# Layer 2 of a four-layer image network, written as two streams instead of one

## The chip, the cores and the metric

The kernel runs on one core of a Trainium2 chip. The metric is the device time of one execution in microseconds (us); smaller is better. Engines are named as in the profile: PE (matrix multiply) and PEld (its weight loads), DVE (vector engine), ACT (activation engine), POOL (GpSimd, which here issues the indirect DMAs), SP (which issues all other DMAs).

## What is computed

Sixteen images of 192 channels and 32x32 pixels pass through four layers, each with a group norm in front and a residual sum behind. Only layer 2, a deformable depthwise convolution, is touched; the others share its engines.

```python
# layer 2: x = x + deform(groupnorm(x))
offset = conv3x3(x, w_off) + b_off            # 18 numbers per pixel: 9 taps, (dy, dx)
py = row + ky + offset[:, :, 0]; px = col + kx + offset[:, :, 1]
for yi, xi, wgt in four_corners(floor(py), floor(px)):   # bilinear sampling
    acc += gather(x, clip(yi) * W + clip(xi)) * (wgt * valid)
out = einsum('bckhw,ck->bchw', acc, w_def)    # 9 taps, one weight per channel and tap
```

Layer 0 is a gated recurrence with a convolution, layer 1 an attention whose queries and keys come from a small simulated circuit, layer 3 a gated feed-forward block with a 2x2 transform and a depthwise 3x3 convolution.

## The kernel before

The small circuit's tables come first, then phase A (layer 0), until about 3290 us. The rest is phase B, where layers 1 to 3 of different images run side by side. It is written as Python generators. Each emits the instructions of its part and now and then yields a number, the planned cost of what it has emitted. `weave` (from line 83) holds for each stream a plan time, starts it at the stream's third number, takes a step of the stream whose plan time is smallest, and adds the step's cost divided by the stream's second number. One unit of plan time is therefore one image in every stream; it is called a *unit* below. The framework's scheduler then orders each engine's queue: the emission order is the priority, and an instruction that is ready while an engine is free may go ahead of one that isn't. On the chip, each queue is in order.

There are four streams in phase B before the change:

- `vectors` (from line 959), 87.0 a unit, start 0: the residual of layer 0, group norm, the circuit's states `psi` (line 1035), `pcirc` (1057), its square `prob` (1059, ACT), `pz` (1069).
- `attention` (1110), 205.8, start 1.27: per pair of heads, `pmax` (1132, PE), its row maxima `mx` (1164, DVE), `pscore` (1132, PE), `pexp` (1206, ACT), `pav` (1196, PE). `pmax`, `pscore`, `pcirc` and layer 3's `phad` share a PSUM tag `big` of two buffers.
- `layer2` (1272), 169.5, start 2.53: for each image first `layer2_offsets`, then `layer2_gathers`, one after the other.
- `layer3` (1435), 136.9, start 3.81: `phad` (1474), the depthwise taps `dc` (1525, DVE), `pout` (1560).

`layer2_offsets` (49.5 of the 169.5 a unit, with 2 for the tail of the image in front) does the group norm, writes the padded image `xpad`, transposes it into five tiles `xt` (1311) and writes these with 22 DMAs (1298) into a DRAM table `xg`, of which there are two, used in turn; `poffc` (1327) is the offset convolution, 72 matmul records an image; then come 15 short DVE instructions that make the row numbers `ix` (1358) and the four corner weights `w4` (1363).

`layer2_gathers` does 36 steps an image (4 blocks of pixels by 9 taps), each planned at 3.0. A step issues two indirect DMAs (`read`, 1382) two steps ahead into `gt` (six buffers, that is three steps), makes the first corner's product of the next step on ACT (`first`, 1390), adds the other three corners with six DVE instructions (1423), multiplies by the weights of the tap (1425), and adds the result into the PSUM tile `pdef` by a matmul with the identity (1429). After the ninth tap a `tail` copies the block out of PSUM (1395), transposes it (`pdt`, 1403), adds the residual (1406) and stores it to `x3d`, from which layer 3 reads. The tail is emitted with the first tap of the next block; that of the last block after the first step of the next image's offsets.

Tags shared by both halves: `acc` with five buffers (for `acc` and for `xt`), PSUM `mm` with two (`pxt`, `poffc`, `poff`, `pdt`, and the small matmuls of the other streams), `xp` with three (`ot`, the tail's `x2`, and layer 3's `tot` and `xo`), `ix` and `w4` with two each.

Of the kernel before, what the change touches and what calls it, by code (L numbers as in the profile page):

```python
# [52 lines left out]
def groupnorm(nc, pool, mm, cn, x, out):  # L53

    gm, rs = yield from groupstats(nc, pool, mm, cn, x)
    nm = pool.tile([96, 2], F32, tag="gnnm", name="gnnm")
    nc.vector.scalar_tensor_tensor(nm, gm, -1.0, rs, ALU.mult, ALU.mult)
    yield 1.5
    for k in range(2):
        xk = x[k] if len(out[k].shape) == 2 else x[k].rearrange("p (r w) -> p r w", w=32)  # L60
        nc.scalar.activation(out[k], xk, AF.Identity, bias=nm[:, k:k + 1], scale=rs[:, k:k + 1])
# [21 lines left out]
def weave(streams):  # L83


    streams = [[s[2] if len(s) > 2 else 0.0, s[1], s[0]] for s in streams]
    while streams:
        s = min(streams, key=lambda s: s[0])
        try:
            s[0] += next(s[2]) / s[1]  # L90
        except StopIteration:
            streams.remove(s)
# [685 lines left out]
def phase_b(tc, d, out, ydram, stats, cn, nb):  # L778

    nc = tc.nc  # L780
    with ExitStack() as ctx:
# [152 lines left out]


        left = [SimpleNamespace() for _ in range(nb)]
        done = [nb] + [0] * 4
        g = SimpleNamespace(**locals())

        def together(n):  # L940
# [5 lines left out]
        def stream(i, work):  # L946
            for b in range(nb):
                assert done[i] > b
                yield from work(g, b, left[b])
                done[i + 1] = b + 1  # L950


        nc.scalar.preload_act_table_set("natural_log_exp_and_others")

        weave([(stream(0, vectors), 87.0), (attention(g), 205.8, 1.27), (layer2(g), 169.5, 2.53),
               (stream(3, layer3), 136.9, 3.81)])


def vectors(g, b, left):
# [309 lines left out]
    yield from todo.ends  # L1269


def layer2(g):
    late = SimpleNamespace(tail=iter(()))
    for b in range(g.nb):
        assert g.done[2] > b
        yield from layer2_offsets(g, b, g.left[b], late)
        yield from layer2_gathers(g, b, g.left[b], late)
    yield from late.tail


def layer2_offsets(g, b, left, late):


    nc, cn, p1, p2, mm = g.nc, g.cn, g.p1, g.p2, g.mm
    xpad, x = g.xpad, left.x
    xg = g.xg[b % 2]
    norm = groupnorm(nc, p2, mm, cn, [x[:, k, :] for k in range(2)],
                     [xpad[:, k, 1:33, 1:33] for k in range(2)])
    yield next(norm)
    yield from late.tail  # L1290
    yield from norm
    yield 2.0

    def table(xt, cr, u, t0, n, q):

        dst = bass.AP(tensor=xg.tensor, offset=xg.offset + (u + 128 * t0 + q) * 768 + cr * 192,
                      ap=[[768, 128 - q], [128 * 768, n], [1, 192]])
        nc.sync.dma_start(dst, xt[q:])


    flat = xpad.rearrange("p k r w -> p k (r w)")
    for t2 in range(5):
        n = min(2, 9 - t2 * 2)
        pv = mm("pxt")
        for j in range(n):
            o = 4 + (t2 * 2 + j) * 128
            for k in range(2):
                nc.tensor.transpose(pv[:, (j * 2 + k) * 96:(j * 2 + k) * 96 + 96], flat[:, k, o:o + 128],
                                    cn.ident[:96, :96])
        xt = g.pairs("xt")  # L1310
        nc.scalar.activation(xt[:, 0:n, :], pv[:, 0:n * 192].rearrange("p (t c) -> p t c", t=n), AF.Identity)
        for cr, sh in enumerate((0, 1, 34, 35)):
            if sh > 4 and t2 == 0:
                table(xt[:, 0:1, :], cr, 4 - sh, 0, 1, sh - 4)
                table(xt[:, 1:2, :], cr, 4 - sh, 1, 1, 0)
            else:
                table(xt[:, 0:n, :], cr, 4 - sh, t2 * 2, n, 0)
        yield 1.5


    po = mm("poffc")
    for t in range(9):
        dy, dx = t // 3, t % 3
        for k in range(2):
            for hf in range(2):
                q = (k * 2 + hf) * 32
                nc.tensor.matmul(po[q:q + 32, :], g.woff[:, k, t, :],  # L1327
                                 xpad[:, k, hf * 16 + dy:hf * 16 + dy + 16, dx:dx + 32], start=(t == 0), stop=(t == 8))
        yield 2.0
    yield 3.0  # L1330
    ot = g.xp("ot")
    nc.scalar.activation(ot, po, AF.Identity)
    yield 2.0
    pf = mm("poff")
    for j in range(4):
        nc.tensor.transpose(pf[:, j * 128:(j + 1) * 128], ot[:, j * 128:(j + 1) * 128], cn.ident)
    yield 4.0
    n = 144
    pos = p1.tile([128, n], F32, tag="pos", name="pos")
    pfv = pf.rearrange("p (j k f c) -> p k f j c", j=4, k=2, f=2)  # L1340
    posv = pos.rearrange("p (f j c) -> p f j c", f=2, j=4)
    nc.vector.tensor_tensor(posv, pfv[:, 0, :, :, 0:18], g.gridb.rearrange("p (f j) c -> p f j c", f=2), ALU.add)
    nc.vector.tensor_tensor(posv, pfv[:, 1, :, :, 0:18], posv, ALU.add)
    nc.vector.tensor_scalar(pos, pos, -1.0, 32.0, ALU.max, ALU.min)
    fi = p1.tile([128, n], I32, tag="fi", name="fi")
    nc.vector.tensor_copy(fi, pos)
    fl = p1.tile([128, n], F32, tag="fl", name="fl")
    nc.vector.tensor_copy(fl, fi)
    t1 = p1.tile([128, n], F32, tag="t1", name="t1")
    nc.vector.tensor_tensor(t1, fl, pos, ALU.is_gt)  # L1350
    nc.vector.tensor_sub(fl, fl, t1)
    nc.vector.tensor_sub(pos, pos, fl)
    nc.vector.tensor_scalar(t1, pos, -1.0, 1.0, ALU.mult, ALU.add)
    flv = fl.rearrange("p (n c) -> p n c", c=2)
    iv = p1.tile([128, n // 2], F32, tag="iv", name="iv")
    nc.vector.scalar_tensor_tensor(iv, flv[:, :, 0], 34.0, flv[:, :, 1], ALU.mult, ALU.add)
    ix = p2.tile([128, n // 2], I32, tag="ix", name="ix")
    nc.vector.tensor_scalar_add(ix, iv, 35.0)
    w4 = p2.tile([128, 4, n // 2], F32, tag="w4", name="w4")
    pv_ = pos.rearrange("p (n c) -> p n c", c=2)  # L1360
    qv_ = t1.rearrange("p (n c) -> p n c", c=2)
    for cr in range(4):
        nc.vector.tensor_mul(w4[:, cr, :], (pv_ if cr // 2 else qv_)[:, :, 0], (pv_ if cr % 2 else qv_)[:, :, 1])
    left.ix, left.w4 = ix, w4
    yield 6.0
# [202 lines left out]
def network(tc, d, out, nb):  # L1568
    nc = tc.nc
    with ExitStack() as ctx:  # L1570
        cp = ctx.enter_context(tc.tile_pool(name="c_1", bufs=1))
        dp = ctx.enter_context(tc.tile_pool(name="c_d", bufs=1, space=DRAM))
        cn = SimpleNamespace()
        cn.ident = load(nc, cp, d["ident"], "ident")
        cn.g6 = load(nc, cp, d["g6"], "g6")
        const_cols(nc, cp, cn, [("eps5", 1e-5), ("one", 1.0), ("lnsc", -0.5 * math.log(32.0)), ("hpi", math.pi / 2)])
        cn.lqk = cp.tile([128, 2, 128], F32, name="lqk")
        ydram = dp.tile([nb, 192, 2, HS], F32, name="ydram")
        stats = dp.tile([192, nb, 2, 6], F32, name="stats")
        circuits(tc, d, cn)  # L1580
        phase_a(tc, d, ydram, stats, cn, nb)
        phase_b(tc, d, out, ydram, stats, cn, nb)
# [126 lines left out]
```

## Time and profile before

| | |
|---|---|
| median of 3 runs | 9260.08 us (9257.92 to 9267.99) |
| the profiled execution | 9279.24 us |
| its span, first to last instruction | 9277.3 us |
| busy over the span: PE, DVE, ACT, POOL | 85%, 75%, 46%, 20% |
| mean granted TensorE clock | 0.847 |
| first gather of image 0, 2, 13, 15 | 3807.3, 4441.5, 8348.7, 8946.7 us |
| last gather issued | 9116.7 us |
| the attention's last `pexp` | 8835 us |

How to read it: the rows by line give an instruction's busy time over the whole execution, the mean duration of one, and after the second bar the idle time of its engine just before it, with what ended that. A row of a stretch gives the stretch (us from the span's start), its length, then the busy time of PE, PEld, DVE, ACT and POOL with the number of instructions, the granted clock, the DMA engines' busy share and GB/s. A row of the waits says which engine and line waited for what, how long in all, how often, and the longest.

From image 2 to image 13 phase B repeats itself: 11 images between 4441.5 and 8348.7 us, 355.2 us each. Within one such period the first gather to the last takes about 247 us (the *gather stage*), and the rest, about 106 us, in which no gather is issued, is the *offset stage*.

### The profile page before, as it was taken

What the parts mean: (1) busy time and instruction counts of PE and PEld (TensorE: products, weight loads), DVE (VectorE), ACT (ScalarE), POOL (GpSimd) and SP (SyncE); (2) the same over time, 40 slices, a digit from 0 to 9 for tenths busy, and PEclk for the clock granted to TensorE, in tenths of its full rate; (3) what the DMA queues carried; (4) which work ended last, traced back from release to release, by engine and by line L of the source; (5) the groups of instructions that cost most, each with busy time, mean ns of one, the idle gap of its engine ahead of it and who ended that gap; (6) DMA issues with size and microseconds to landing.
All of it is one profiled execution on the core that took longest, in us unless ns stands there. A gap on an engine that the chain in (4) does not pass through costs nothing. (4 is left out here: it accounts for less than half of the span.)

```text
span 9277.3 us, 92108 instructions
## 1 busy us (share of the span) xinstructions
PE 7898.9 (85%) x30512; PEld 3406.5 (37%) x30512; DVE 6930.6 (75%) x14313; ACT 4241.6 (46%) x7405; POOL 1851.5 (20%) x1680
## 2 busy tenths in 40 slices
PE   5999999999999959898888888888888888888843
PEld 2555555555555532233323223323323233232221
DVE  7777777777777743569778778778788778788888
ACT  3444444444444424445444444444444445454432
POOL 0100000101010000222312223223223223223242
PEclk9899999999999968887887888877887878878865
DMA  1111111111111110433333433434334334334342
GB/s 53 42 40 45 47 47 43 45 43 46 44 50 43 42 49 19 132 119 118 121 118 104 127 116 116 124 113 124 114 120 124 110 107 136 109 106 138 121 152 68
DMA packets 303530, 819.62 MB, mean 88 GB/s; under 512 B 48827, under 2 KB 165629, under 8 KB 303051
## 3 DMA queue, kind: packets, MB, share of 16 engines
q0 software_dynamic: 92160, 453.06, 15.7%
q1 hardware_dynamic: 210891, 360.67, 12.9%
q8 instruction: 240, 3.93, 0.2%
q14 instruction: 239, 1.96, 0.1%
HBM read 667.52 MB, written 132.94 MB: 86 GB/s over the span
## 5 line engine op out<-in xcount | busy, mean ns | idle before, releaser
L1382 POOL DMA_INDIRECT gt<-xg,ix x1152 | 1529.3, 1328 | 4259.5 <-DVE acc L1423 1496.2
L1423 DVE SCALAR_TENSOR_TENSOR acc<-gt,w,acc 128x192 f32<-128x192 f32 x3456 | 1210.0, 409 | 246.9 <-ACT acc L1390 243.3
L1132 PE MATMUL pmax<-kt,qt 32*128 32x512 f32 x3072 | 996.4, 863 | 256.4 <-ACT pexp L1206 226.1
L1164 DVE TENSOR_REDUCE mx<-pmax 128x2 f32<-128x1024 f32 x768 | 922.7, 1217 | 328.1 <-PE pmax L1132 327.1
L1390 ACT ACTIVATE acc<-gt,w 128x192 f32<-128x192 f32 x1152 | 503.3, 451 | 1307.6 <-DMA gt<-xg,ix 1084.4
L1196 PE MATMUL pav<-pexp,vo 128*64 128x512 f32 x3072 | 1032.0, 713 | 11.7 <-ACT pexp L1206 11.7
L1206 ACT ACTIVATE pexp<-pscore 128x1024 f32<-128x1024 f32 x768 | 767.6, 1015 | 481.5 <-PE pscore L1132 348.0
L1132 PE MATMUL pscore<-qt,kt 32*128 32x512 f32 x3072 | 807.9, 731 | 166.6 <-DVE mx L1164 105.2
L509 POOL COPY qbd<-qT 32x384 f32<-32x384 f32 x512 | 305.4, 596 | 2838.9 <-PE se L543 2752.1
L1429 PE MATMUL pdef<-acc,ident 128*128 128x384 f32 x1152 | 660.4, 664 | 206.2 <-DVE acc L1425 206.2
L1525 DVE SCALAR_TENSOR_TENSOR dc<-pad,wdw,dc 128x512 f32<-128x512 f32 x1152 | 804.6, 742 | 26.3 <-ACT dc L1523 25.1
L539 ACT ACTIVATE dm<-dm,wtm 128x128 f32<-128x128 f32 x1536 | 490.7, 388 | 347.2 <-DVE dm L495 267.5
L1132 PEld LDWEIGHTS pmax<-kt,qt 32*128 32x128 f32 x3072 | 281.2, 240 | 856.7 <-ACT pexp L1206 458.2
L551 PEld LDWEIGHTS pintra<-v,pt 128*128 128x128 f32 x3072 | 426.0, 212 | 163.3 <-issue 70.0
L1429 PEld LDWEIGHTS pdef<-acc,ident 128*128 128x128 f32 x1152 | 214.7, 231 | 703.4 <-DVE acc L1425 329.9
L1132 PEld LDWEIGHTS pscore<-qt,kt 32*128 32x128 f32 x3072 | 224.9, 204 | 648.2 <-DVE mx L1164 294.3
L551 PE MATMUL pintra<-v,pt 128*128 128x33 f32 x3072 | 435.3, 290 | 2.5 <-DVE pt L546 2.3
L1059 ACT ACTIVATE prob<-pcirc 128x1024 f32<-128x1024 f32 x192 | 195.9, 1023 | 510.2 <-PE pcirc L1057 499.6
L1196 PEld LDWEIGHTS pav<-pexp,vo 128*64 128x64 f32 x3072 | 202.1, 154 | 588.9 <-issue 558.8
L1057 PE MATMUL pcirc<-psiT,lqk 64*128 64x512 f32 x768 | 312.6, 788 | 97.3 <-DVE mx L1164 72.5
L546 DVE SCALAR_TENSOR_TENSOR pt<-se,dm 128x512 f32<-128x512 f32 x384 | 262.9, 685 | 141.1 <-PE se L543 138.0
L1560 PE MATMUL pout<-gelu,wout 128*96 128x512 f32 x512 | 267.7, 673 | 87.0 <-DVE gelu L1548 79.7
(423 smaller groups left out, 12887.5 us busy)
## 6 DMA issues: line engine op xcount, KB each, us to landing
dm<-gd SPq DMA_DIRECT2D x128, 768.0 KB
xg<-xt SPq DMA_DIRECT2D x224, 192.0 KB
gt<-xg,ix POOLq DMA_INDIRECT x1152, 4.5
xb<-x_in SPq DMA_DIRECT2D x32, 384.0 KB
y<-ydram SPq DMA_DIRECT2D x32, 384.0 KB
x1d<-xb SPq DMA_DIRECT2D x32, 384.0 KB
xnd<-y SPq DMA_DIRECT2D x32, 384.0 KB
xn<-xnd SPq DMA_DIRECT2D x48, 256.0 KB
```

The lines of the kernel that those rows point to most:

```text
L539: nc.scalar.activation(dm[:, h, :], dm[:, h, :], AF.Exp, bias=wtm[:, c, 64 + h:65 + h])
L551: nc.tensor.matmul(pa[:, hh * 33:hh * 33 + 33], pt[:, h * 128:(h + 1) * 128], v33[:, hh, :], start=True, stop=True)
L1057: nc.tensor.matmul(pc[:, hh * HS:(hh + 1) * HS], cn.lqk[r, w, :], ps[hf][r, :], start=True, stop=True)
L1132: nc.tensor.matmul(out[j][:, hh * HS:(hh + 1) * HS], lhs(j, r), rhs(j, r), start=True, stop=True)
L1164: nc.vector.tensor_reduce(mx[:, tt, hf, :], pm[hf].rearrange("p (h s) -> p h s", h=2), AX.X, ALU.max, negate=True)
L1196: nc.tensor.matmul(po[0][hh * 64:hh * 64 + 64], vo[:, tt, hh * 32:hh * 32 + 64], pe[:, hh * HS:(hh + 1) * HS], start=(tt == 0), stop=(tt = ...
L1206: nc.scalar.activation(pe, ps[j], AF.Exp)
L1382: nc.gpsimd.indirect_dma_start(out=gt, out_offset=None, in_=xg, in_offset=bass.IndirectOffsetOnAxis(ap=ix[:, c:c + 1], axis=0))
L1390: nc.scalar.activation(acc[:, j, :], gt[:, 0:192], AF.Copy, scale=w4[:, 0, c:c + 1])
L1423: nc.vector.scalar_tensor_tensor(acc[:, j, :], gt[:, cr * 192:(cr + 1) * 192], w4[:, cr, c:c + 1], acc[:, j, :], ALU.mult, ALU.add)
L1429: nc.tensor.matmul(po[:, 0:384], cn.ident, acc.rearrange("p j c -> p (j c)"), start=(t == 0), stop=(t == 8))
L1525: nc.vector.scalar_tensor_tensor(out, src, w, add, ALU.mult, ALU.add)
```

## The change

`layer2` becomes two streams. `offsets` runs `layer2_offsets` image by image; its 49.5 are followed by empty steps of 1.0 up to 140.5, so that its unit is again one image and its work lies in the first 0.352 of the unit. `gathers` runs `layer2_gathers` image by image with 120 a unit: 4 + 36 x 3 + 4 tails x 2. It starts 0.38 units behind `offsets`. The tail of an image's last block is now emitted with the first tap of the next image. `layer3` starts at 3.96 instead of 3.81. No instruction is added or removed.

```diff
-        done = [nb] + [0] * 4
+        done = [nb] + [0] * 5
...
-        weave([(stream(0, vectors), 87.0), (attention(g), 205.8, 1.27), (layer2(g), 169.5, 2.53),
-               (stream(3, layer3), 136.9, 3.81)])
+        weave([(stream(0, vectors), 87.0), (attention(g), 205.8, 1.27), (offsets(g), 140.5, 2.53),
+               (gathers(g), 120.0, 2.91), (stream(3, layer3), 136.9, 3.96)])
...
-def layer2(g):
+def offsets(g):
+
+    for b in range(g.nb):
+        assert g.done[2] > b and g.done[3] + 2 > b
+        spent = 0.0
+        for cost in layer2_offsets(g, b, g.left[b]):
+            spent += cost
+            yield cost
+        g.done[5] = b + 1
+        while spent < 140.0:
+            spent += 1.0
+            yield 1.0
+
+
+def gathers(g):
     late = SimpleNamespace(tail=iter(()))
     for b in range(g.nb):
-        assert g.done[2] > b
-        yield from layer2_offsets(g, b, g.left[b], late)
+        assert g.done[5] > b
         yield from layer2_gathers(g, b, g.left[b], late)
     yield from late.tail
...
-def layer2_offsets(g, b, left, late):
+def layer2_offsets(g, b, left):
...
-    yield next(norm)
-    yield from late.tail
     yield from norm
     yield 2.0
```

## The prediction, made before the changed kernel was run

> **What bounds the kernel now.** I began with the slices of the whole span, to find the part that repeats.
>
> ```profile
> PE   5999999999999959898888888888888888888843
> DVE  7777777777777743569778778778788778788888
> PEclk9899999999999968887887888877887878878865
> ```
>
> Slices 17 to 37 are one flat stretch, PE at eight to nine tenths and DVE at seven to eight: neither is full, so the two hold each other up. Next I cut periods into the stage with gathers and the stage without, and beside these put the first image, at which layer 3 does not run yet, and the end.
>
> ```profile
> 3807.00:4002.00 195.00, 166.32 (x531) 54.51 (x532) 146.84 (x332) 86.10 (x146) 84.58 (x71) 0.75 0.53 165
> 4002.00:4100.00 98.00, 94.34 (x477) 31.53 (x474) 51.76 (x96) 52.52 (x73) 0.99 (x2) 0.97 0.27 79
> 5161.00:5407.00 246.00, 199.19 (x709) 74.42 (x710) 203.22 (x428) 121.40 (x205) 92.21 (x72) 0.83 0.46 140
> 5407.00:5513.00 106.00, 100.27 (x389) 30.84 (x390) 77.75 (x138) 51.24 (x64) 0.61 (x1) 0.81 0.24 71
> 8835.00:9128.00 293.00, 132.22 (x356) 59.22 (x356) 244.89 (x558) 95.89 (x184) 157.53 (x92) 0.60 0.49 154
> ```
>
> In the gather stage (third row) PE is busy 0.81 and DVE 0.83; in the offset stage (fourth) PE 0.95 and DVE 0.73. So the offset stage is PE's, and the gather stage nobody's. What waits in it is in the waits of the third row's stretch, and of the fourth's:
>
> ```profile
> ACT acc L1390 <- DMA gt<-xg,ix: 59.2, 35, 6.2
> PE pmax L1132 <- ACT pexp L1206: 17.3, 6, 5.9
> DVE acc L1423 <- ACT acc L1390: 16.3, 7, 6.3
> ```
>
> ```profile
> DVE psi L1035 <- issue: 19.9, 1, 19.9
> PEld pmax L1132 <- ACT pexp L1206: 3.8, 4, 1.5
> ```
>
> In the gather stage ACT stands 59.2 us with `first` at the head of its queue until a gather lands; `pexp` is queued behind it, and PE's largest wait is for `pexp`. In the offset stage that wait is nearly gone, and DVE stands 19.9 us in one piece while PE runs `poffc`, `pcirc` and `pz` without a gap. The rows by line say that this hole comes in most images (321.0/16 = 20 us) and that POOL's long idle time is mostly behind DVE's tap sums, whose buffers the gathers reuse:
>
> ```profile
> L1035 DVE TENSOR_TENSOR psi<-vec 128x512 f32<-128x512 f32 x96 | 62.2, 686 | 321.0 <-issue 224.8 <-PE pz L1069 80.7 <-ACT gelu L1546 15.4
> L1382 POOL DMA_INDIRECT gt<-xg,ix x1152 | 1529.3, 1328 | 4259.5 <-DVE acc L1423 1496.2 <-DMA qt<-qt 1361.6 <-DVE w L1363 526.8
> ```
>
> **What is moved.** Nothing is added or removed; only places change. One period of gathers, by the rows by line over 16 images: DVE (1210.0 for L1423 + 317.1 for L1425)/16 = 95.4 us, ACT 503.3/16 = 31.5 for L1390, PE 660.4/16 = 41.3 for L1429. Before, they lie in 0.708 of a unit (120/169.5), now in all of it. So 0.292 of them goes from the gather stage to what was the offset stage: DVE 27.9, ACT 9.2, PE 12.1 us.
>
> *What the offset stage pays.* The first image gives prices. From the second row to the fourth, layer 3 adds DVE 26.0 and PE 5.9 us, and the time grows by 8. DVE's share was free; PE's cost 1.36 for one. The moved PE work costs 12 us at one for one, 16 at 1.36. DVE then has 77.75 + 27.9 = 105.7 us; at the 0.83 of the gather stage, the densest steady stretch, that needs 128 us, 22 more than now. The hole takes some of it: at 9.9 us a step (355.2/36) two steps, 5.3 us of DVE, more if later steps go ahead. Ends 12 and 22; I take 17, near the PE price, to which the rows are nearest.
>
> *What the gather stage gets back.* From the first row to the third, layer 3 adds DVE 56.4, PE 32.9 us, and the time 51: 0.90 per us of DVE, 1.55 per us of PE. Taking 27.9 of DVE away gives 25, taking 12.1 of PE away 19 (12 at one for one). Beside that a step grows from 6.9 us (247/36) to 9.9. A step's two gathers must be issued (92.21/72 = 1.28 us each in the third row) and land (4.5 us median from issue), about 7.1 us, between one step's release of `gt` and the `first` that reads it, about one step of emission. At 6.9 that is late, at 9.9 early: the 59.2 us should go, and up to 17.3 us of PE's wait with them. What is late next is `mx`, for which `pscore` waits. Ends 12 and 25 + 17 = 42; I take 28, the DVE price and a little of the wait, since part of the wait is in the price already.
>
> *Two tags shared.* `xt` takes slots of the five of `acc` while gathers run. A tile is held for four DMA issues of 0.47 us and a landing (nearest row: 4.5 for a gather), 6.4 us, and five follow each other at 1.5/140.5 of a period, 3.8 us: two of them and two or three `acc` just fill the five. A `first` that found none would hold ACT, with `pexp` behind it, then PE: from 0 to 5 x 2.6 = 13 us; I take 0 to 2, inside the 17. `poffc` holds one of two `mm` for 21/140.5 of a period instead of 21/169.5, 53 us instead of 44, and one of four tails now falls into it, but `pout`, four `mm` tiles, moves out of it with layer 3's 0.15: taken as even, between -3 and 3.
>
> *The queues.* SP keeps its 22 table writes and the tails' loads and stores in another mix; it is 22 x 0.47 = 10 us of issue. POOL's gathers are now at its head while `ix` of the next image is made; these are planned 0.07 units (25 us) ahead of the first gather, so POOL should not stand for them. The 111.5 us that it now stands each period is no cost and goes.
>
> *Table writes beside gathers.* DMA engines are 0.46 busy in the gather stage and 0.24 without gathers, which sums to less than one; I count nothing. The Trainium skill (Trainium Kernel Development and Optimization, Key Constraints) says that transfers from SP, ACT and POOL run on the same 16 engines and interleave, which speaks against the change. If landing doubled for the three steps or so beside the writes, the 7.1 would be 11.6 against 9.9, 5 us a period and some 65 in all; no row shows it.
>
> *Gather issues beside dense DVE work.* Median 1.00, but in each steady image one issue lasts 7.9 us, while DVE runs `tot`, `dc` and tap sums without a pause, and near the end 13.0. The Trainium skill (GPSIMD Engine Reference, Key points) says why: POOL shares its SBUF interfaces with DVE, and instructions with two SBUF inputs contend. Half of layer 3's dense stretches lay where no gather was issued; now all meet them. One or two more such issues, each 6.9 long less the 2.8 of slack (9.9 - 7.1), would be 4 to 8 us a period; this is part of the slower rival.
>
> *Ends.* `gathers` finish at plan time 18.91 instead of 18.53, layer 3 0.15 later. When the attention ends (17.27), 0.64 + 1 images of gathers are left instead of 0.37 + 1, and 0.15 images more of layer 3, whose DVE work an image is about 83 us ((804.6 + 91.0 + 84.4 + 83.3 + 82.2 + 78.0 + 109.7)/16): 26 + 12 = 38 us of DVE more. There DVE is the bound (244.89 of 293, fifth row): 38/0.83 = 46 us later. At the start the same work is missing, but PE bounds there, and it loses 11 + 5 us: 16 to 25 us sooner. Together 22 later, between 10 and 46.
>
> **Sum.** A period: +17 - 28 = -11 us (ends: 12 - 42 = -30, 22 - 12 = +10). Thirteen periods (4157 us, layer 3's first `phad`, to 8835, divided by 355): -143. With +22: -121, so the profiled execution goes from 9279.24 to 9158. The median of the runs is 0.998 of that execution: 9140 us. Its own ends: -390 + 10 gives 8880, and a steady gain of only 3 us a period 9240.
>
> **Rivals.**
> 1. *Gathers fill every hole.* PE comes to the 0.95 of the offset stage everywhere. For: the hole is at DVE just where the taps are missing. Against: `pdef`, `pscore` and `pmax` wait for DVE and ACT, `poffc` for nobody. 299.5 us of PE a period / 0.946 = 317, 35 less than 352: -455 + 22, or 8830.
> 2. *DVE becomes the bound where PE was.* Place: the stretch with `poffc`; outside its hole DVE is already busy 77.75 of 86 us. There the 27.9 us cost 22, plus 6 for stretched gather issues, while the gather stage, limited by PE and the two `big` buffers, gives back 12 to 20. It decides from where the stretch loses more than the other gives, that is if less than the price of PE's waits returns. At +10 a period: +130 + 22, 9410 us: slower.
> 3. *The taps do not spread.* The scheduler runs what is ready: `had` (L1448) of the next image runs at 5479, ahead of the `xo` (L1553) of this one at 5508, against emission order. If it bunches the taps again as far as `gt` allows, or steady gain and ends cancel, 9255.
>
> **Chances.** The sum 0.50, rival 1 0.10, rival 2 0.30, rival 3 0.10. A measurement of this kernel tells apart about 0.2%, here 19 us. Faster: 0.47 of the sum's cases, 0.10 of rival 1, 0.01 of rival 3: 0.58. Same: 0.03 + 0.05 = 0.08. Slower: 0.30 + 0.04 = 0.34. The likeliest one's own range is 8880 to 9240; to hold 8 in 10 it reaches up to rival 2 and leaves rival 1 out: 8900 to 9420.
>
> **What would show it.** In the profile of the changed kernel: a steady period near 344 us; gathers at an even 9 to 10 us a step with no pause at POOL of 100 us; ACT's wait for landings down from 59 to under 20 us a period; DVE's hole before `psi` filled; PE near 0.88. Wrong if PE waits more for `mx` or for `pdef`'s `acc`, if `first` waits for a table write, if gather issues of 7 us come several times an image, or if the last 440 us grow by more than 50.

## The result and the profile after

| | before | after |
|---|---|---|
| median, beside each other on one chip (4 runs each) | 9259.0 us | 9372.04 us (9352.33 to 9380.02) |
| ratio, with its 95% interval | | 1.0122 (1.0098 to 1.0146) |
| the profiled execution, and its span | 9279.24, 9277.3 us | 9365.61, 9363.8 us |
| first gather of image 2, of image 13 | 4441.5, 8348.7 us | 4450, 8419 us |
| steady period (the difference of these / 11) | 355.2 us | 360.8 us |
| the attention's last `pexp` to the end | 442 us | 501 us |

The forecast was 9140; the kernel became 1.2% slower. *Before* and *after* name the two kernels from here on. The two spans differ by 86.5 us: 8 up to the first gather of image 2, 62 in eleven steady periods, 16 from image 13 to the end. In after, the lines of layers 2 and 3 stand 11 further on (L1401 is the old L1390).

The slices of the whole span, from the page of after:

```profile
PE   5999999999999969888888888888888888888843
...
DVE  7777777777777734568778778778778777788878
...
PEclk9899999999999978888887877887887877878865
```

The picture is the old one: a flat stretch, PE at 8, DVE at 7 to 8. PEclk is hardly lower: eight sevens in slices 17 to 37, where there were seven. The steady stretch of before, then that of after with the first 293 us after the attention's end (length; busy PE, PEld, DVE, ACT, POOL; granted clock, DMA share, GB/s):

```profile
4441.00:8349.00 3908.00, 3356.49 (x12076) 1195.01 (x12078) 3095.43 (x6219) 1899.40 (x2949) 1020.97 (x793) 0.81 0.39 118
```

```profile
4450.00:8419.00 3969.00, 3386.84 (x12069) 1175.17 (x12065) 3094.05 (x6215) 1925.02 (x2981) 1188.07 (x793) 0.80 0.38 116
8863.00:9156.00 293.00, 131.76 (x351) 59.60 (x351) 234.40 (x532) 90.26 (x170) 181.15 (x93) 0.61 0.48 151
```

The counts and DVE's busy time are the same. PE's share is 0.853 (3386.84/3969), not 0.88. PE is busy 30 us longer for the same matmuls, and idle 31 us longer. POOL, which only issues gathers, is busy 167 us longer. The last row reads as that of before did (DVE 244.89 of 293): the end is still DVE's.

Now the waits over the steady stretch (total, times, longest). Before:

```profile
ACT acc L1390 <- DMA gt<-xg,ix: 724.7, 426, 6.2
...
DVE psi L1035 <- issue: 200.9, 11, 20.8
PE pmax L1132 <- ACT pexp L1206: 185.9, 75, 7.2
...
PE ppsi L1046 <- DVE xo L1553: 82.7, 11, 8.6
```

After:

```profile
ACT acc L1401 <- DMA gt<-xg,ix: 772.7, 326, 11.3
POOL gt L1393 <- issue: 471.6, 299, 31.9
POOL gt L1393 <- ACT acc L1401: 460.5, 55, 40.9
...
ACT acc L1401 <- PE pdef L1440: 177.5, 44, 9.0
...
DVE xo L1564 <- PE pout L1571: 138.5, 33, 7.3
...
DVE x L1417 <- PE pdt L1414: 135.2, 33, 7.1
...
PE pmax L1132 <- ACT pexp L1206: 97.4, 84, 4.1
...
PE pscore L1132 <- ACT pexp L1206: 69.2, 23, 5.8
PE pscore L1132 <- ACT kt L1121: 64.4, 11, 6.3
```

Two things went as planned: DVE's hole before `psi` is gone, and PE's wait of `pmax` for `pexp` is halved. But ACT's wait for landings, which was to fall to under 20 us, is 772.7/11 = 70.2 us a period instead of 65.9. PE has new waits for the same ACT (`pscore` for `pexp`, for `kt`), and DVE waits in layer 3's last sum (`xo`) and in layer 2's residual (`x`) for PE, 12 us a period each, which were 0.2 and 0.3 before. The timeline of POOL at the start of an image (start, duration, idle time before):

```profile
5554.64 0.95 POOL L1393 DMA_INDIRECT gt<-xg,ix  x1 [0.30 <-issue]
5594.15 1.00 POOL L1393 DMA_INDIRECT gt<-xg,ix  x1 [38.57 <-ACT acc L1401]
```

The steps of an image are not even. In the image whose gathers begin at 5531 us, the first eight pairs of gathers start 0, 2, 5, 9, 12, 15, 19 and 22 us after it, as fast as `gt` allows; the ninth comes at 63. Before, in the image at 5513 us, the first eight started at 0, 3, 5, 8, 14, 17, 25 and 29, and the ninth at 40. The rows of the gathers over the steady stretch (min/median/max in ns), before and after:

```profile
L1382 POOL DMA_INDIRECT gt<-xg,ix x793: 943/1000/7921, 4441.5 to 8348.7; - x199
```

```profile
L1393 POOL DMA_INDIRECT gt<-xg,ix x793: 940/998/13008, 4449.9 to 8419.0; - x199
```

The median issue is as before; the long ones, over 3 us, went from 2.0 to 5.3 a period. Is one of these what made the period longer?

### The profile page after: what moved, and what is told of

The parts are those of the page before. It is cut to its first block, busy times and chain, and to the rows that moved or that the text cites. A ratio compares the mean times of both kernels' runs of the same rounds, so it can differ in the third digit from the quotient of the medians.

```text
span 9363.8 us, 92166 instructions
## 1 busy us (share of the span) xinstructions
PE 7941.4 (85%) x30512; PEld 3381.7 (36%) x30512; DVE 6930.1 (74%) x14313; ACT 4272.1 (46%) x7442; POOL 2063.2 (22%) x1680
## 5 line engine op out<-in xcount | busy, mean ns | idle before, releaser
L1393 POOL DMA_INDIRECT gt<-xg,ix x1152 | 1742.2, 1512 | 4152.9 <-DVE acc L1434 1342.5
L1132 PE MATMUL pscore<-qt,kt 32*128 32x512 f32 x3072 | 883.3, 754 | 329.1 <-DVE mx L1164 121.8
L1132 PE MATMUL pmax<-kt,qt 32*128 32x512 f32 x3072 | 970.3, 824 | 223.8 <-ACT pexp L1206 123.3
L1401 ACT ACTIVATE acc<-gt,w 128x192 f32<-128x192 f32 x1152 | 493.2, 451 | 1409.1 <-DMA gt<-xg,ix 1145.7
L1196 PE MATMUL pav<-pexp,vo 128*64 128x512 f32 x3072 | 1054.2, 735 | 4.9 <-ACT pexp L1206 3.8
L1206 ACT ACTIVATE pexp<-pscore 128x1024 f32<-128x1024 f32 x768 | 771.4, 1016 | 587.3 <-PE pscore L1132 368.4
L509 POOL COPY qbd<-qT 32x384 f32<-32x384 f32 x512 | 304.2, 594 | 2836.5 <-PE se L543 2749.8
L1536 DVE SCALAR_TENSOR_TENSOR dc<-pad,wdw,dc 128x512 f32<-128x512 f32 x1152 | 804.0, 747 | 18.3 <-ACT dc L1534 17.9
L1440 PE MATMUL pdef<-acc,ident 128*128 128x384 f32 x1152 | 635.0, 640 | 174.7 <-DVE acc L1436 174.7
L1132 PEld LDWEIGHTS pmax<-kt,qt 32*128 32x128 f32 x3072 | 259.5, 229 | 786.7 <-ACT pexp L1206 371.9
L1440 PEld LDWEIGHTS pdef<-acc,ident 128*128 128x128 f32 x1152 | 210.6, 227 | 613.5 <-issue 321.0
L1485 PE MATMUL phad<-had,win 96*128 96x256 f32 x1024 | 334.6, 489 | 61.3 <-ACT pexp L1206 54.2
L546 DVE SCALAR_TENSOR_TENSOR pt<-se,dm 128x512 f32<-128x512 f32 x384 | 263.2, 685 | 140.8 <-PE se L543 137.8
L1057 PE MATMUL pcirc<-psiT,lqk 64*128 64x512 f32 x768 | 273.2, 795 | 103.3 <-ACT pexp L1206 59.9
L543 PE MATMUL se<-qbd,kT 64*128 64x256 f32 x1536 | 290.4, 447 | 54.9 <-DVE pt L546 54.9
```

The source lines that it names most:

```text
L1132: nc.tensor.matmul(out[j][:, hh * HS:(hh + 1) * HS], lhs(j, r), rhs(j, r), start=True, stop=True)
L1196: nc.tensor.matmul(po[0][hh * 64:hh * 64 + 64], vo[:, tt, hh * 32:hh * 32 + 64], pe[:, hh * HS:(hh + 1) * HS], start=(tt == 0), stop=(tt = ...
L1206: nc.scalar.activation(pe, ps[j], AF.Exp)
L1393: nc.gpsimd.indirect_dma_start(out=gt, out_offset=None, in_=xg, in_offset=bass.IndirectOffsetOnAxis(ap=ix[:, c:c + 1], axis=0))
L1401: nc.scalar.activation(acc[:, j, :], gt[:, 0:192], AF.Copy, scale=w4[:, 0, c:c + 1])
L1440: nc.tensor.matmul(po[:, 0:384], cn.ident, acc.rearrange("p j c -> p (j c)"), start=(t == 0), stop=(t == 8))
```

## The experiments

The prediction had priced layer 3's later start only at the ends. So the experiments move layer 3 and layer 2 apart from each other. A *place* below is the fraction of a unit at which layer 3 starts: .81 before, .96 after. All times in us; the ratio is to the kernel before, run beside it; the last three columns are per steady period. *Half clock* is the time in which the granted clock was 0.5. A period is that of one profiled execution. Nineteen executions of before, run beside e1 to e5, took from 9245.90 to 9292.29 us; if all of such a difference lay in the eleven steady periods it would be 4.2 us in each (an estimate), so a difference of periods under that is not shown by one pair of profiles.

| kernel | time | ratio (95%) | period | PE busy | PE idle | half clock |
|---|---|---|---|---|---|---|
| before (one stream, .81) | 9259.0 | | 355.2 | 305.1 | 50.1 | 134.4 |
| e1 one stream, .96 | 9396.74 | 1.0142 (1.0119 to 1.0165) | 364.8 | 294.6 | 70.2 | 127.8 |
| e6 one stream, .10 | 9067.3 | 0.9791 (0.9774 to 0.9807) | 336.9 | 282.5 | 54.4 | 110.1 |
| e5 two streams, not spread, .81 | 9274.81 | 1.0013 (0.9999 to 1.0026) | 353.0 | 301.8 | 51.2 | 133.7 |
| e2 two streams, .81 (a unit later) | 9259.54 | 0.9991 (0.9977 to 1.0004) | 347.2 | 300.8 | 46.4 | 117.6 |
| after (two streams, .96) | 9372.04 | 1.0122 (1.0098 to 1.0146) | 360.8 | 307.9 | 52.9 | 142.4 |
| e3 two streams, .10 | 9056.9 | 0.9772 (0.9750 to 0.9794) | 333.6 | 287.3 | 46.3 | 103.1 |
| e7 two streams, .30 | 9432.45 | 1.0178 (1.0158 to 1.0198) | 368.4 | 309.9 | 58.5 | 145.8 |
| e11 two streams, .43 | 9319.58 | 1.0075 (1.0054 to 1.0095) | 358.0 | 296.2 | 61.9 | 137.4 |
| e12 two streams, .62 | 9213.83 | 0.9954 (0.9941 to 0.9968) | 345.9 | 301.5 | 44.4 | 122.2 |
| e9 after, `pdt` in `pdef`'s bank | 9336.46 | 1.0084 (1.0062 to 1.0106) | 357.5 | 304.5 | 53.0 | 127.2 |
| e10 the same, .10 | 9066.51 | 0.9786 (0.9766 to 0.9805) | 336.0 | 292.5 | 43.6 | 107.1 |
| e13 after, `pout` halved | 9306.12 | 1.0052 (1.0025 to 1.0078) | 354.5 | 304.2 | 50.3 | 146.8 |
| e14 the same, .10 | 9003.74 | 0.9729 (0.9704 to 0.9754) | 330.1 | 282.4 | 47.7 | 108.6 |
| e15 layers 2 and 3 later by 0.14 | 9330.49 | 1.0080 (1.0050 to 1.0111) | 353.5 | 308.7 | 44.8 | 132.7 |
| e18 after, `poffc` cut to 2 of 9 taps | 9240.11 | 0.9982 (0.9964 to 1.0000) | 351.8 | 301.6 | 50.2 | 140.8 |
| e19 the same, .10 | 9007.98 | 0.9732 (0.9685 to 0.9780) | 329.2 | 281.4 | 47.8 | 112.6 |

### The parts of the change: layer 3's place (e1, e2, e3)

e1 does in the kernel before only what the diff does to layer 3. e2 and e3 keep the two streams and move layer 3: e2 back to the old place (one unit later), e3 on by 0.14.

```diff
-               (stream(3, layer3), 136.9, 3.81)])
+               (stream(3, layer3), 136.9, 3.96)])     e1, from before
-               (gathers(g), 120.0, 2.91), (stream(3, layer3), 136.9, 3.96)])
+               (gathers(g), 120.0, 2.91), (stream(3, layer3), 136.9, 4.81)])     e2, from after
+               (gathers(g), 120.0, 2.91), (stream(3, layer3), 136.9, 4.10)])     e3, from after
```

> The kernel before with one number changed: layer 3 starts at 3.96 instead of 3.81; layer 2 stays one stream. Theory A (collision): in the changed kernel layer 3's four pout tiles and the tail of an image's last block fall together on the two mm buffers; here the tails keep their places, and the last tail (plan time .53) is far from pout (.90 to .96), so the period stays at 355 us within 3 and the time at 9260 to 9320 (0.15 units later end). Theory B (phase): the shift of layer 3 against the attention and the vectors is by itself what costs; then the period is about 361 here too, and the time 9340 to 9400. Theory C (taps): the taps beside the offsets cost, the shift nothing: like A here, 355.

> The changed kernel with layer 3 a further 0.85 units later, at 4.81: in the steady part it stands against the attention and the vectors as it did before the change, and pout lies at .75 to .81 of a unit, away from every tail (.19, .43, .67, .94). The end is about 0.85 units of layer 3 longer, which costs some 100 us or more, so the steady period is what is read. Theory A: period 350 to 356. Theory B: 350 to 356 too. Theory C: 361 as in the changed kernel.

> The changed kernel with layer 3 at 4.10 instead of 3.96, so that pout is planned at .04 to .10, between the tails at .94 and .19; its place against attention and vectors is new. Theory A: DVE's waits for pout and pdt (25 us a period in the changed kernel) fall under 5, the pause of the gathers near the image's start goes, period 350 to 356, time 9260 to 9330. Theory B: any period, no link with pout and pdt. Theory C: period 361, waits of ACT for landings unchanged near 70 us.

The steady stretches, e1:

```profile
4458.00:8471.00 4013.00, 3240.40 (x12067) 1150.94 (x12067) 3101.19 (x6216) 1870.38 (x2938) 1076.84 (x792) 0.82 0.38 115
```

e2:

```profile
4412.00:8232.00 3820.00, 3308.98 (x12071) 1162.87 (x12067) 3089.14 (x6219) 1922.32 (x2959) 1214.59 (x792) 0.83 0.41 120
```

e3:

```profile
4442.00:8112.00 3670.00, 3160.44 (x12069) 1124.73 (x12071) 3088.83 (x6218) 1919.71 (x2981) 1083.64 (x792) 0.85 0.42 125
```

e1 alone costs 9.6 us a period (364.8 - 355.2), and its time is above that of after. In two streams the same move costs 13.6 (360.8 - 347.2). At a fixed place the two streams are no slower: their period is 4.0 shorter at .96 (364.8 - 360.8), as much as one execution can differ, and 8.0 at .81 (355.2 - 347.2). So the loss is layer 3's move and not the spreading. Theory C falls with all three runs; A had e1 at 355, and e3's 333.6 is far under its 350. Under B, e1 came about as expected, while e2's 347.2 is below the 350 that A and B both gave. e2's time is nevertheless that of before: its period gains 88 us in eleven, and its end takes 141 more (583 against 442 after the attention), since a unit more of layer 3 is left. e3 beats both kernels by over 2%.

What the move does in one stream is in PE's own waits (that of `pmax` for `pexp` before was shown above, 185.9), before and then e1:

```profile
PE pscore L1132 <- DVE mx L1164: 62.8, 81, 1.9
...
PE paug L1120 <- ACT pexp L1206: 7.4, 6, 1.8
```

```profile
PE pmax L1132 <- ACT pexp L1206: 276.0, 121, 6.0
PE paug L1120 <- ACT pexp L1206: 142.8, 11, 13.1
PE pscore L1132 <- DVE mx L1164: 131.1, 118, 4.0
```

Once an image PE now stands 13 us at `paug`, and the attention waits longer for ACT and DVE. These three waits grow by 12.3, 8.2 and 6.2 us a period, 26.7 together; less the `ppsi` wait that is no longer among the large ones (82.7/11 = 7.5) that is 19.2, nearly the 20.1 that PE is idle longer (70.2 - 50.1). The period grew by only 9.6 of these, since PE was busy 10.5 us less (305.1 - 294.6) for the same matmuls: its busy time at half clock fell from 121.6 to 100.0.

### The split without the spread (e5)

Both streams get 169.5 a unit, the gathers come right behind the offsets, as in one stream, and wait out the next image's offsets; layer 3 at .81.

```diff
-        weave([(stream(0, vectors), 87.0), (attention(g), 205.8, 1.27), (offsets(g), 140.5, 2.53),
-               (gathers(g), 120.0, 2.91), (stream(3, layer3), 136.9, 3.96)])
+        weave([(stream(0, vectors), 87.0), (attention(g), 205.8, 1.27), (offsets(g), 169.5, 2.53),
+               (gathers(g), 169.5, 2.83), (stream(3, layer3), 136.9, 3.81)])
...
-        while spent < 140.0:
+        while spent < 169.0:
...
-    yield from late.tail
+        yield from late.tail
+        late.tail = iter(())
+        for i in range(99):
+            yield 0.5
```

> Two streams as in the changed kernel, but the taps are not spread: both have 169.5 a unit, gathers start at 2.83 and end the image with its last tail and 49.5 of empty steps, layer 3 starts at 3.81. It is the plan of the kernel before, written as two streams. Theory C: with the taps taken back from beside the offsets, period 355, time 9240 to 9290. Theories A and B say the same, since no tail meets pout and layer 3 is where it was. If it is 361, then the split itself costs, and all three fall.

353.0 a period and 1.0013 of the time: the restructuring itself costs nothing. The 2.2 us between 353.0 and 355.2 is no gain that is shown: the profiled execution of e5 was the fastest of its ten (9252.04 of up to 9295.62).

### Is layer 3's place good or bad without the two streams (e6)

```diff
-               (stream(3, layer3), 136.9, 3.81)])
+               (stream(3, layer3), 136.9, 4.10)])
```

> The kernel before with layer 3 at 4.10 instead of 3.81, nothing else. The periods so far: 355.2 before, 364.8 with layer 3 at 3.96, and with two streams 347.2 (4.81), 360.8 (3.96), 333.6 (4.10). Theory B (the place of layer 3 within the unit sets most of it, and the spread taps gain 4 to 8 us at any place): period 338 to 346, time 9080 to 9170. Theory D (the good place is good only because the taps leave it free, so the gain belongs to the spread): period 352 or more, time 9260 or more.

```profile
4443.00:8149.00 3706.00, 3107.83 (x12067) 1121.54 (x12067) 3091.77 (x6224) 1880.40 (x2949) 1054.07 (x792) 0.84 0.40 124
```

One number in the kernel before, and 18.3 us a period are gone (355.2 - 336.9). The place .10 is good with one stream and with two; the 3.3 that the two streams add (336.9 - 333.6) is within what one execution can differ. Theory D falls; the period is a little under B's 338.

### Is it the tail beside `pout` (e7, e9, e10)

Theory A was that in after the tail's `pdt` and layer 3's `pout` meet on the two `mm` buffers: the new waits of `x` and `xo`, and the pause of 40 us behind the eighth step, fit it. e7 moves layer 3 further off; e9 and e10 give `pdt` the bank of `pdef` instead of `mm`, at .96 and at .10.

```diff
-               (gathers(g), 120.0, 2.91), (stream(3, layer3), 136.9, 3.96)])
+               (gathers(g), 120.0, 2.91), (stream(3, layer3), 136.9, 4.30)])     e7
-        pt = mm("pdt")[:96].rearrange("p (k s) -> p k s", k=2)
+        pt = g.pp.tile([128, 512], F32, tag="pdef", name="pdt", bufs=1)[:96].rearrange("p (k s) -> p k s", k=2)     e9, e10
```

> The changed kernel with layer 3 at 4.30: pout is planned at .24 to .30, again between two tails (.19, .43). Theory A (a tail beside pout on the two mm buffers is what costs): as good as 4.10, period 330 to 338. Theory B (layer 3's whole load against the attention's and the vectors'): its own value, anywhere from 333 to 361.

> The changed kernel, layer 3 at 3.96 as in the change, but the tail's transposes go into the PSUM bank of pdef, which df has just emptied, and no longer into one of the two mm buffers that pout, pz and pzt want at that time. Theory A: DVE's 25 us a period of waits for pout and pdt shrink to under 12, period 345 to 353, time 9160 to 9270. Theory B: the tail is not what layer 3 collides with, period 357 to 362, time 9340 to 9390.

> The same with layer 3 at 4.10. Theory A: little to gain, since pout and the tails are apart there: period 331 to 336, time 9040 to 9080. Theory B: the same. If it is slower than 9100, the next block's first matmul, which now waits until DVE has read the bank, costs more than the mm buffer did.

```profile
4435.00:8488.00 4053.00, 3408.95 (x12073) 1190.53 (x12069) 3097.74 (x6221) 1917.77 (x2970) 1279.12 (x792) 0.80 0.36 114
```

That is e7's steady stretch: the worst of all, 368.4, where A had expected a period as good as at .10 and B had named 361 as the highest. With `pdt` off `mm` the period at .96 falls by 3.3 only (357.5), and 21.5 of the 27.2 us between .96 and .10 remain (357.5 - 336.0). DVE's waits for `pout` and `pdt` stay at 24.6 us a period there (122.6 and 148.1 in eleven), where A had them under 12, and e7 has only 8.9 of them (2.5 and 94.9). A falls. The pause behind the eighth step is in e2 too, at 347.2.

### More places (e11, e12)

Theory E: `pout` and the attention's three groups of pairs repeat with a third of a unit, so places a third behind .10 should be good again.

```diff
-               (gathers(g), 120.0, 2.91), (stream(3, layer3), 136.9, 3.96)])
+               (gathers(g), 120.0, 2.91), (stream(3, layer3), 136.9, 4.43)])     e11
+               (gathers(g), 120.0, 2.91), (stream(3, layer3), 136.9, 4.62)])     e12
```

> The changed kernel with layer 3 at 4.43. Collisions with tails have fallen as a cause. Theory E: what counts is where pout (the last 0.058 of layer 3's unit, PE's densest piece) stands against the attention, which repeats three times a unit: its pairs start at .07, .40 and .74, and at a start it sends paug and pv but no pmax with its row maxima. Layer 3's start modulo a third was .10 (333.6 and 336.9 us), .14 (347.2, 355.2), .29 (360.8, 364.8), .30 (368.4). 4.43 is .10 again: period 332 to 342, pout 19 to 22 us long. Theory F (the vectors or the offsets, which come once a unit, decide): nothing repeats after a third, and the period is anywhere, 345 to 368 being the more likely.

> The changed kernel with layer 3 at 4.62, that is .29 modulo a third, like 3.96. Theory E: period 357 to 368, pout near 30 us. Theory F: anywhere, no link with 3.96.

358.0 at .43, 345.9 at .62: no thirds. At .43 `pout` takes 20.1 us from the start of its first matmul to that of its last (mean of images 3 to 10), as at .10 (19.5), where after has 30.7; a short `pout` does not make a short period. E falls, and with it `pout` as a mark of the cause.

### `pout` and `poffc` made shorter (e13, e14, e18, e19)

If one of the two PE blocks that layer 3 meets were the place of the loss, the distance between .96 and .10 would shrink when that block does.

```diff
-            for i in range(4):
+            for i in range(0, 4, 3):     pout: e13 at .96, e14 at .10
-        for k in range(2):
+        for k in range(2 if t % 8 == 0 else 0):     poffc: e18 at .96, e19 at .10
```

> The changed kernel at 3.96 with pout cut to two of its four matmuls (it leaves out half of layer 3's last sum); PE loses 8 us a period. If pout's place is what costs 27 us between 3.96 and 4.10, it costs half as much now: period 340 to 346 here, and 12 to 16 above the next run. If layer 3's depthwise taps, not pout, stand wrongly at 3.96, the period falls by 8 or less, to 353 to 357, and the distance to the next run stays at 25 or more.

> The same cut at 4.10: 326 to 331 under both, since pout was 19.5 us of gapless PE there and half of it goes.

> The changed kernel at 3.96 with poffc cut to the first and the last of its nine taps (it leaves out seven ninths of the offset convolution; PE loses 8 us a period, and the mm buffer is planned to be held as long). Theory G in the form 'layer 3's taps beside poffc's dense matmuls': period 336 to 345, within 15 of the next run. If poffc is not it: 350 to 356, and 22 or more above the next run.

> The same cut (seven ninths of the offset convolution left out) with layer 3 at 4.10: a period of 325 to 330 us under both theories, since only the removed PE work is saved.

The distance is 24.4 with a short `pout` (354.5 - 330.1) and 22.6 with a short `poffc` (351.8 - 329.2), of 27.2. Neither block's length is where most of the loss lies. Half of `pout` and two ninths of `poffc` still run there.

### What does layer 3 collide with (e15)

Layers 2 and 3 start 0.14 later together: layer 3 stands to layer 2 as in after, to the attention and the vectors as in e3.

```diff
-        weave([(stream(0, vectors), 87.0), (attention(g), 205.8, 1.27), (offsets(g), 140.5, 2.53),
-               (gathers(g), 120.0, 2.91), (stream(3, layer3), 136.9, 3.96)])
+        weave([(stream(0, vectors), 87.0), (attention(g), 205.8, 1.27), (offsets(g), 140.5, 2.67),
+               (gathers(g), 120.0, 3.05), (stream(3, layer3), 136.9, 4.10)])
```

> The changed kernel with layer 2 and layer 3 both 0.14 later: offsets 2.67, gathers 3.05, layer 3 4.10. Layer 3 stands against the attention and the vectors as in the run at 4.10 (333.6 us a period), and against layer 2 as in the changed kernel (360.8). Theory G (layer 3's taps are slow beside layer 2's offsets, whose poffc, pxt and tables lie at .53 to .88 in the changed kernel; half an image of taps that falls there takes 150 us, elsewhere 110 to 135): period 355 to 365. Theory H (layer 3 against the attention and the vectors): 331 to 341.

353.5, between the ranges of G and H: of the 27.2 us 7.3 come back, 20 stay. That speaks for layer 3's place beside layer 2 as the larger part, but layer 2 has moved against the attention as well, and its share can't be taken out. The converse (layer 2 earlier, or the vectors alone moved) was not run.

## Why the prediction was wrong, point by point

**The step that failed** is the one that took layer 3's 0.15 as free in the steady part. The prediction has it as "`pout`, four `mm` tiles, moves out of it with layer 3's 0.15: taken as even, between -3 and 3", and otherwise only under the ends. By itself it costs 9.6 us a period, 106 in eleven. With the -4.0 of the two streams at that place this gives the +5.6 that after shows. All the rest of the working was on layer 2. `poffc`'s hold of an `mm` buffer, in the same term, was mis-sized too: from its first matmul to the end of its copy out it is 30.6 us before and 61.5 after (images 3 to 10), where the prediction has 44 and 53; but at 57.5 in e3 it doesn't make the difference between the places.

**The net of -11 a period** had the right sign for the two streams alone and was too large: -4.0, -8.0 and -3.3 at the three places at which both forms ran, the first and the last no larger than what one execution can differ; its range was -30 to +10. With the old place, as in e2, the steady gain is -88 in eleven periods.

**ACT's wait for landings** was to fall from 59.2 to under 20 us, because a step would take 9.9 us. It is 70.2: the steps are not 9.9 apart but bunched. The tap sums lie in the plan evenly; on the chip the first eight steps go ahead in 22 us and a pause of 41 follows. This is the ground of rival 3, which was weighed at a tenth. In e3 the wait is 41.8 (459.9/11), still over twice the figure.

**The hole of DVE** is filled, as said: the idle time before `psi` fell from 321.0 to 64.6 us in the rows by line. The step was right, and it buys less than its size: the hole was 20 us an image, and the two streams gain 8.0 at the old place.

**The shared `acc`.** ACT's `first` now waits for a buffer that `pdef` frees 177.5/11 = 16.1 us a period, where it had 7.9 (87.2/11): 8.2 more, inside the bound of 13, over the 0 to 2 taken. It doesn't decide the time: in e3 it is 32.0 (352.0/11).

**POOL.** The pause of 100 us is gone; the longest are now 41 and 32. Even steps were not seen. The prediction put POOL's idle time before the change mostly down to DVE's tap sums; its row says 1496.2 of 4259.5 us, about a third.

**Table writes beside gathers** cost nothing that the record shows: where the trace has a gather's landing in the steady stretch, its median is 4.6 us from issue before and 4.5 after.

**Gather issues beside dense DVE work** are as the slower rival had it: POOL's busy time is 15.2 us a period more, the longest issue 13.0. But e2 has more of it (1214.59/11 = 110.4 a period against 108.0) and a period of 347.2, and e3's longest is 18.5; a larger share of such issues doesn't go with a longer period. That DVE's work is what lengthens an issue was not tested.

**The ends** were put at +22 (10 to 46). The first gather of image 2 comes 8 later, not 16 to 25 sooner; from image 13 to the end it is 16 more; together 25. The stretch behind the attention grew by 59, over the 50 that was named as a sign of error. The sum of this term held by luck, since its parts didn't.

**The rivals.** Rival 2 gave 9410, which is near the time, by another cause: in the stretch of `poffc`, where DVE was to be the bound, it is busy 0.82 in after and PE 0.91 (first to last matmul, images 3 to 10). Rival 1 did not come: PE is at 0.853, not 0.95.

**What is open.** Which instructions of layer 2, or which together, make one place of layer 3 dear and another cheap. What can be said is where the time is in the records. In the two-stream kernels, half an image of layer 3's depthwise taps (first `oe` to the next `phad` or `pout`, mean of images 3 to 10) takes 109 to 135 us in e2, e3 and e12, but about 150 where it meets all of the offsets' `pxt` and `poffc` and 132 us or more of the stretch of the vectors' `pcirc`: 153 for the second half in after, 150 and 154 for the first in e7 and e11 (141 for the second in e15, which meets 99 us of it). In e3 the halves take 119 and 133. DVE, which does these taps, is busy 0.76 of the 153 us and 0.87 of the 133, so the longer half is not one in which DVE is full. This mark fails with one stream: in e1 it is the first half that takes 146 us (125 before), and it meets neither `pxt` nor `poffc`.

## What to carry to other kernels

When an edit also moves a stream's start, run that move alone, in the old kernel: here a side number cost 9.6 us of every period, and the redesign it came with gained at most 4 there and 8 at the old place. In a kernel woven from streams that repeat, try the starts before a redesign: from .30 to .10 the same instructions took 368.4 and 333.6 us a period, and one number in the kernel before gave -2.1%. Price a spread by what the queues allow, not by the plan: work that is planned evenly but is ready early runs early.

## What the runs showed of the hardware

**PE's busy time is not its work.** The clock record of PE has two levels, full and half. In the steady stretch of after the median `pav` matmul took 592 ns at full clock and 1112 at half. If, as an estimate, the busy time at half clock counts half, PE's work a period is 244 us before, 243 after, 239 in e3 and 245 in e7 (305.1, 307.9, 287.3 and 309.9 busy). So the 27.2 us between after and e3 are 4 of work, 16.5 of half clock (busy at half clock 130.1 and 97.0, half of the difference) and 6.6 of idle time. More idle time does not always bring more time at half clock: e1 has 20.1 us more of the one than before, and 6.6 less of the other (127.8 against 134.4).

**What lowers it.** The half-clock stretches last a multiple of 3.41 us, 3.4 to 20.5 in after. In the steady stretch of after such a stretch began during or within 2 us behind each of the 49 pauses of PE of 3 us or more, and behind 51 of the 116 of 1 to 2 us. In e1 it was 61 of 79 pauses of 3 us or more; at the other 18 the clock was at half already. After has 4.5 pauses of 3 us or more a period, e3 2.2. The Trainium skill (TensorE: Matmul & The Clock Gate, Part 1: The HAM clock gate) says that the clock drops to half after an idle window of about 3.4 us, which the long pauses bear out. But of the 142 us a period at half clock in after only 33 lie in stretches that began at such a pause; in the 7 us ahead of a stretch PE was idle 28% in the median, against 15% over the period (52.9/360.8). So most of the half-clock time here came without such a window, and the measurement decides. What share of idle time is enough was not measured. The pauses don't explain the places by themselves: e6 has 5.4 of them a period at 336.9 us.
